# A group-routed residual MLP: dropping reader-less products and laying out every engine's list anew

## The chip, the core and the metric

The kernel runs on one core of a Trainium2 chip. A core has five engines, each with its own queue of instructions, taken in order: TensorE (PE) multiplies matrices, VectorE (DVE) and ScalarE (ACT) work elementwise, GpSimd (POOL) does elementwise work and issues the gathers, and SyncE (SP) issues plain copies (DMA). Engines wait for one another by semaphores. PE writes its products into PSUM, eight banks of 128 x 512 float32 here, which the other engines read. The metric is the device time of one execution, in microseconds (us). Three runs of the kernel before gave 941.57, 938.49 and 941.36 us, median 941.36.

## The reference

There are 16 x 512 = 8192 tokens of width 512. Every token is normalised in several ways, the results are joined and go through a two-layer MLP with a norm behind it, and the input is added:

```python
h = _ln(x, pw_g[pathway_ids], pw_b[pathway_ids])        # gain and bias from one of 500 rows
h = _ln(h, cp_g[compartment_ids], cp_b[compartment_ids])  # of 5 rows
t = _ln(x, tm_g[time_steps], tm_b[time_steps])            # of 5 rows, same ids
m = x + _mlp_ln(memory_state, ...)[:, None, :]            # one row per batch entry
n = x + _mlp_ln(noise_state, ...)[:, None, :]
r = x + _mlp_ln(resource_state, ...)[:, None, :]
s = _ln(x, ms_g[scale_type], ms_b[scale_type])            # scale_type is a 0/1 mask
w = jax.nn.softmax(aw)
cat = jnp.concatenate([w[0]*h, w[1]*t, w[2]*m, w[3]*n, w[4]*r, w[5]*s], axis=-1)
return x + _mlp_ln(cat, int_W1, int_b1, int_W2, int_b2, int_g, int_be)
```

All products are float32, and PE takes a float32 product in two records.

## The kernel before

The tokens are sorted by their group (the pair of time and scale ids) and worked through in 16 tiles of 512 tokens, each four row tiles of 128. The 3072-wide first layer is folded: the parts that are x itself times some weight are summed into one weight (the X block, `wx_`), the two table norms t and s into one weight for each group (the V block, `vs`, rebuilt by ACT and DVE where a row tile's group differs from the one before), and h has its own weight (the H block, `wh_`). The bias rows come from a gather.

For one tile the steps are these. Names such as `q7.p.0.5` are pieces: a kind, the tile, and numbers of a row tile, a pair of row tiles or a product.

- x, h's gain and bias, a compartment row and the bias rows are gathered by POOL (`gx`, `gh`, `gc`, `ga`). ACT and DVE normalise (`xs`, `nv`, `f1`, `fs`, `f2`, `fn`).
- DVE transposes x, v and h in 32 x 32 squares (`tx`, `tv`, `th`, into rX, rV, rH), and SP spreads these to full 128 x 128 transposes by plain copies (`sX`, `sV`, `sH`, four copies for each of four rows, L198) into the turned columns cX, cV, cH.
- PE multiplies: `lV` is the V block of one row tile (8 records of 128 x 512, L392). X and H together are seven half products for each pair of row tiles (`m7.c.pair.1` to `7`, 8 records of 128 x 256 each, L440), after the scheme that saves one product in eight. It needs sums of columns by DVE (`u1` to `u4`, L421 to L427) and sums of products by DVE (`r1`, `r2`, `r3`, `r5`, L451 to L457), which add PSUM banks to the gathered bias rows.
- `ha` (DVE, L460) and `hs` (ACT, silu) make the hidden row tiles; `tz` and `sZ` turn them into cZ.
- The second layer is seven products for each pair of row tiles too (`q7`, L543), with column sums by POOL (`zs`) and sums of products by ACT and DVE (`kf`, `ku`, `sf`, `sl`). Then follow the squares (`lq`), a power by POOL (`lp`), scale and residual (`lb`, two DVE passes, L629 and L630) and the indirect write (`po`, POOL, L634). The last tile takes a plain second layer (`l2`, L475) and a square root on ACT (`sd`, `rv`, `ft`).

The order on every engine is written out by hand in three strings of pieces: ORDER (the head: load, the three conditioning MLPs, tile 0, whose columns PE itself flips, pairs of rows called extras, and the first steps of tile 1), WINDOW (run for tile 0 to 14; p, c, n, m are the tile before, this one, the next and the one after it) and LAST (tile 15). A piece's instructions go to their engines in the order of the strings, nothing is reordered later.

`awake` (L395 to L401) emits a product of 128 x 512 of a weight with itself into a bank that a later product of the list clears. Nothing reads its result. ORDER calls it twelve times, as `wu.lX.0.1.n` into the bank of tile 0's row tile 1 (nine times) and as `wu.ex.n.m` into an extra's bank (three times).

The turned columns live in a pool with one buffer for each of the four blocks. A tile takes the buffer anew at its first copy (`spread_row`, `flipped`, `flipped_extra`), and the head uses parts of it as scratch (`flat_cat`).

## Time and profile before

| | |
|---|---|
| median of three runs | 941.36 us |
| span of the profiled execution | 935.9 us |
| PE busy | 909.9 us, 97% |
| DVE, ACT, POOL busy | 745.0, 502.1, 655.0 us |
| dense products of tile 0 begin | 80.07 us |
| first window's first product | 146.11 us |
| second window | 198.5 to 249.1 us |
| last window's first product | 861.63 us |
| last product ends | 928.1 us |

The time of a run is the span and what lies around it; the profiled execution is shown with its span only, which is 5.5 us under the median. Times inside it count from its start. In the profile a line such as L392 is the line of the kernel, `p<-vs,cV` says what is written and read, and "idle before <-" names what ended an engine's wait. Several parts of one instruction's operands can share a line, since a piece of all tiles has one line. PEclk is the granted clock of PE, as a share of full speed.

### The profile page before, as it was taken

How to read it: one execution, taken by the hardware profiler on the slowest of the kernel's cores; microseconds unless marked ns; L12 is line 12 of the kernel's file. 1: busy time of each engine (PE TensorE's matmuls, PEld its weight loads, DVE VectorE, ACT ScalarE, POOL GpSimd, SP SyncE). 2: the span in 40 equal slices, each digit the busy share in tenths (PEclk: the TensorE clock that was granted, in tenths of full speed). 3: DMA queues.
4: the chain of work that ended last, by engine and by line, in shares of the span. 5: the costliest groups of instructions: out<-in, count | busy, mean ns of one | idle time of the engine just before them, and what ended most of it. 6: DMA issues, size and time to landing. Idle time of an engine off the chain costs nothing. (4 is left out here: it accounts for less than half of the span.)

```text
span 935.9 us, 13631 instructions
## 1 busy us (share of the span) xinstructions
PE 909.9 (97%) x3711; PEld 649.5 (69%) x3711; DVE 745.0 (80%) x1359; ACT 502.1 (54%) x1211; POOL 655.0 (70%) x705
## 2 busy tenths in 40 slices
PE   7999999999999999999999999999999999999996
PEld 6734444877768786868687786878686777767673
DVE  8756776887879697979788786979798987889575
ACT  5557855446372737564654628274656466473322
POOL 9566577667777777677687777776777777775533
PEclk9799999999999999999999999999999999999999
DMA  8856677686867777676868686777777786866613
GB/s 277 256 183 192 181 226 196 185 238 167 247 170 237 189 209 208 194 207 201 237 181 250 165 240 176 219 208 209 204 195 214 201 234 164 247 166 180 185 46 99
DMA packets 88861, 186.68 MB, mean 199 GB/s; under 512 B 24372, under 2 KB 24372, under 8 KB 88780
## 3 DMA queue, kind: packets, MB, share of 16 engines
q0 software_dynamic: 31376, 106.19, 39.9%
q1 hardware_dynamic: 56700, 79.50, 29.2%
q8 instruction: 31, 0.51, 0.3%
q14 instruction: 50, 0.41, 0.1%
q10 hardware_dynamic: 704, 0.08, 0.1%
HBM read 101.78 MB, written 19.94 MB: 130 GB/s over the span
## 5 line engine op out<-in xcount | busy, mean ns | idle before, releaser
L392 PE MATMUL p<-vs,cV 128*128 128x512 f32 x504 | 226.3, 596 | 4.0 <-ACTq L237 2.3
L392 PEld LDWEIGHTS p<-vs,cV 128*128 128x128 f32 x504 | 95.9, 191 | 108.5 <-issue 89.5
L339 ACT ACTIVATE junk<-pw 128x512 bf16<-128x512 f32 x60 | 37.7, 629 | 175.2 <-DVE pw L336 84.9
L440 PE MATMUL p<-wh__80,cH 128*128 128x256 f32 x480 | 111.1, 379 | 0.0
L164 POOL DMA_INDIRECT xbs<-in_x,tok x64 | 69.2, 1081 | 44.4 <-DVE yb L630 24.7
L440 PEld LDWEIGHTS p<-wh__80,cH 128*128 128x128 f32 x480 | 91.2, 190 | 12.4
L634 POOL DMA_INDIRECT out<-yb,tok x64 | 65.4, 1023 | 41.8 <-issue 29.2
L164 POOL DMA_INDIRECT pw<-in_pw,i_pw x64 | 64.7, 1010 | 39.0 <-DVE rH L190 19.9
L164 POOL DMA_INDIRECT cp<-cp_rows,i_cp x64 | 78.8, 1231 | 17.5 <-issue 12.2
L380 POOL TENSOR_TENSOR xbs<-xbs,rows 128x512 f32<-128x512 f32 x64 | 82.2, 1286 | 1.2
L164 POOL DMA_INDIRECT add<-rows,i_add x64 | 67.0, 1048 | 14.7 <-issue 12.5
L361 POOL TENSOR_TENSOR rsh<-veh,mhalf 128x1 f32<-128x1 f32 x64 | 49.2, 768 | 37.2 <-DVE veh L357 32.4
L365 ACT ACTIVATE pw<-pw,rsh 128x512 f32<-128x512 f32 x64 | 44.8, 717 | 53.8 <-issue 23.7
L463 ACT ACTIVATE add<-add 128x512 f32<-128x512 f32 x64 | 38.5, 626 | 63.8 <-DVE add L460 45.4
L335 DVE SCALAR_TENSOR_TENSOR pw<-xbs,sums,pw 128x512 f32<-128x512 f32 x60 | 53.6, 893 | 18.5 <-DMA pw<-in_pw,i_pw 16.2
L372 DVE SCALAR_TENSOR_TENSOR pw<-pw,sumsh,cp 128x512 f32<-128x512 f32 x60 | 44.5, 748 | 18.7 <-DMA cp<-cp_rows,i_cp 7.8
L190 DVE STREAM_TRANSPOSE rH<-pw 128x512 f32<-128x512 f32 x60 | 41.3, 703 | 20.5 <-ACT pw L365 19.8
L440 PE MATMUL p<-wt,cH 128*128 128x256 f32 x240 | 56.7, 379 | 0.0
L440 PE MATMUL u<-wt,ss 128*128 128x256 f32 x240 | 54.5, 380 | 0.4 <-DVE add L454 0.4
L440 PE MATMUL u<-wt,cX 128*128 128x256 f32 x240 | 54.4, 380 | 0.0
L440 PEld LDWEIGHTS u<-wx__79,cX 128*128 128x128 f32 x240 | 45.6, 190 | 12.6 <-issue 5.0
L440 PE MATMUL u<-wx__79,cX 128*128 128x256 f32 x240 | 54.2, 379 | 0.0
(428 smaller groups left out, 2124.2 us busy)
## 6 DMA issues: line engine op xcount, KB each, us to landing
cZ<-rZ SPq DMA_DIRECT2D x256, 64.0 KB
cX<-rX SPq DMA_DIRECT2D x240, 64.0 KB
cV<-rV SPq DMA_DIRECT2D x240, 64.0 KB
cH<-rH SPq DMA_DIRECT2D x240, 64.0 KB
w1x<-in_int_W SPq DMA_DIRECT2D x2, 1024.0 KB
rows<-adde SPq DMA_DIRECT2D x14, 128.0 KB
yb<-in_int_W SPq DMA_DIRECT2D x1, 1024.0 KB
ws<-in_int_W SPq DMA_DIRECT2D x1, 1024.0 KB
```

What stands on the lines that cost most here:

```text
L164: nc.gpsimd.indirect_dma_start(dst, None, table, bass.IndirectOffsetOnAxis(ap=idx, axis=0), **kw)
L190: nc.vector.transpose(rot[:, :, :, j, :].rearrange("p q c t -> p c q t"), src.rearrange("p (c q t) -> p c q t", c=NC, q=Q))
L335: nc.vector.scalar_tensor_tensor(h, st["xb"][:, j, :], st["sums"][:, 1, j : j + 1], h, ALU.add, ALU.mult)
L339: nc.scalar.activation(junk, x, AF.Identity, accum_out=sums[:, 0, k : k + 1])
L361: nc.gpsimd.tensor_tensor(rs, st.pop(("ve", j)), mhalf[:, :1], ALU.pow)
L365: nc.scalar.mul(pw[:, :D], pw[:, :D], st.pop(("rs", j)))
L372: nc.vector.scalar_tensor_tensor(pw[:, :D], pw[:, :D], st["sh", j][:, 1], cp, ALU.add, ALU.mult)
L380: nc.gpsimd.tensor_add(st["xb"][:, j, :], st["xb"][:, j, :], rows[:, 2, :])
L392: nc.tensor.matmul(st["p1", g], st["c" + blk][:, g, c, :], m[:, c, :], start=(blk == first and c == 0), stop=(blk == last and c == NC - 1) ...
L440: nc.tensor.matmul(dst, m[:, c], at_["half1"][k][:, c], start=(k == 1 and c == 0), stop=(c == NC - 1), skip_group_check=True)
L463: nc.scalar.activation(st["add", g], st["add", g], AF.Silu)
L634: nc.gpsimd.indirect_dma_start(out_rows[j], bass.IndirectOffsetOnAxis(ap=tok[:, j, w : w + 1], axis=0), yb[:, j, :], None)
```

## The change

Three things are changed.

1. The twelve `wu` pieces leave ORDER. `awake` stays in the file and is not called.
2. The turned columns are four fixed buffers `cats[blk]` instead of tiles of the pool. A first copy of a tile into the buffer had to wait for all readers of the old tile; a copy into a fixed buffer waits for those of the part it overwrites.
3. ORDER, WINDOW and LAST hold the same pieces as before (but for the twelve) in another order.

```diff
 ORDER = """
-    wk.1.2 h2.1 fx dk lt pk bx sz wk.1.1 by kd wu.lX.0.1.0 xs.0.0 xt.0.0 tk tt wk.1.3 wk.2.1 gx.e0.0 xv.0.0
-    wu.lX.0.1.8 lw fg lo xs.0.1 fl.2 wm.4 h2.2 gx.e0.1 wu.lX.0.1.1 fl.1 scl he.1 xt.0.1 ax he.2 gx.e0.3 gx.e0.2 ac
...
+    wk.1.3 cv wk.1.1 bx fx lt pk h2.1 h2.2 lo by kd tk fg dk wk.1.0 se fl.1 wk.1.2 ax h2.0 dp xt.0.1 tt he.1 fl.2
+    ac he.2 he.0 wm.4 dc xv.0.1 gx.e0.0 xs.0.0 pwi eh.2 gx.e0.1 eh.0 gx.e0.2 sz eh.1 wk.2.3 xs.e0.0 xs.0.1 xs.0.2
...
@@ -145,6 +145,7 @@
     yb = const.tile([P, NJ, D], F32, name="yb")
+    cats = {blk: const.tile([P, Q, NC, P], F32, name="cat" + blk) for blk in "XHVZ"}
     rows = const.tile([P, 3, D], F32, name="rows")
@@ -193,7 +194,7 @@
         if cat not in st:
-            st[cat] = catp.tile([P, Q, NC, P], F32, tag=f"cat{blk}", name=f"{cat}{st['w']}")
+            st[cat] = cats[blk]
@@ -646,7 +647,7 @@
     def flat_cat(blk, name):
-        return catp.tile([P, Q, NC, P], F32, tag=f"cat{blk}", name=name).rearrange("p g c t -> p g (c t)")
+        return cats[blk].rearrange("p g c t -> p g (c t)")
@@ -1118,7 +1119,7 @@
         if "c" + blk not in st:
-            st["c" + blk] = catp.tile([P, Q, NC, P], F32, tag="cat" + blk, name=f"c{blk}{st['w']}")
+            st["c" + blk] = cats[blk]
@@ -1281,7 +1282,7 @@
         if "cE" not in st:
-            st["cE"] = catp.tile([P, Q, NC, P], F32, tag="cat" + "ZX"[k // Q], name="cE" + st["w"])
+            st["cE"] = cats["ZX"[k // Q]]
```

The first place is PE's list in the head, around the turn of the conditioning rows (`pt`), the flips of tile 0 (ptX, ptV) and the conditioning product (`pb`). Before, with the products without a reader (awake):

```order
L401 MATMUL awake_lX_1_563<-wt 128x512
L1211 MATMUL pt<-ident,room_114 128x96 x4
L1117 MATMUL ptX_784<-ident,xbs_90 128x128 x4
L1117 MATMUL ptV_795<-ident,xm_1_765 128x128 x4
L401 MATMUL awake_lX_1_563<-wt 128x512
L1222 MATMUL pb<-yb,room_115 32x512 x4
L1222 MATMUL pb<-w1x_136,room_115 32x512 x4
L1222 MATMUL pb<-w1x_137,room_115 32x512 x4
L1117 MATMUL ptV_821<-ident,xm_2_772 128x128 x4
L401 MATMUL awake_ex_834<-wt 128x512
L1117 MATMUL ptV_845<-ident,xm_0_803 128x128 x4
L1254 MATMUL pr_864<-br,pick 120x512
```

and after the change (lines are one higher there, and the scratch that was `room` is now a part of a fixed buffer, catZ or catH):

```order
L1183 MATMUL pb<-ident,room_118 32x128 x4
L276 UNCONDITIONAL_BRANCH x2
L1212 MATMUL pt<-ident,room_118 128x96 x4
L1118 MATMUL ptX_757<-ident,xbs_90 128x128 x4
L1118 MATMUL ptV_771<-ident,xm_1_745 128x128 x4
L1118 MATMUL ptV_776<-ident,xm_2_739 128x128 x4
L1061 TENSOR_LOAD some
L1223 MATMUL pb<-yb,catZ 32x512 x4
L1223 MATMUL pb<-catH,catZ 32x512 x4
L1223 MATMUL pb<-w1x_139,catZ 32x512 x4
L1118 MATMUL ptV_838<-ident,xm_3_812 128x128 x4
L1118 MATMUL ptV_843<-ident,xm_0_819 128x128
```

The three products without a reader are gone, and three flips of tile 0 stand in one row ahead of the conditioning product.

The second place is SP's list where the head ends and the first window begins: cX and cV are tile 1's turned columns, `rows_78<-adde` are the extras' row copies, and the branches belong to parts that run only for a changed group. Before:

```order
L1311 DMA rows_78<-adde_1290 64x512 x2
L1311 DMA rows_78<-adde_1161 64x512 x2
L198 DMA cX_1389<-rX_1138 32x512
L237 UNCONDITIONAL_BRANCH
L198 DMA cX_1389<-rX_1138 32x512 x4
L237 UNCONDITIONAL_BRANCH
L198 DMA cX_1389<-rX_1138 32x512 x7
L198 DMA cV_1474<-rV_1298 32x512 x7
L237 UNCONDITIONAL_BRANCH x2
L198 DMA cV_1474<-rV_1298 32x512
L237 UNCONDITIONAL_BRANCH
L198 DMA cV_1474<-rV_1298 32x512 x3
```

and after:

```order
L1312 DMA rows_78<-adde_1366 64x512
L238 UNCONDITIONAL_BRANCH x2
L1312 DMA rows_78<-adde_1366 64x512
L238 UNCONDITIONAL_BRANCH
L199 DMA catV<-rV_1327 32x512 x9
L238 UNCONDITIONAL_BRANCH
L199 DMA catV<-rV_1327 32x512 x6
L238 UNCONDITIONAL_BRANCH
L199 DMA catV<-rV_1327 32x512
L199 DMA catX<-rX_1084 32x512
L238 UNCONDITIONAL_BRANCH
L199 DMA catX<-rX_1084 32x512 x7
```

Twelve copies of cX stood ahead of the first copy of cV; now all sixteen copies of cV stand ahead of the last eight of cX.

The third place is DVE's list in the window of tile 2, from the last of the output pairs (yb, lines 629 and 630, in the new file 630 and 631) to the sum r2 into add_0 (line 451, new 452). u_0 is the bank that the first pair's products 1, 6 and 7 share; catX and catH are written by the token sums u3 and u4, pw is the next tile's h. Before:

```order
L453 TENSOR_TENSOR add_0_2032<-add_0_2032,u_0_1994 128x256
L454 TENSOR_TENSOR add_1_2126<-add_1_2126,u_0_1994 128x256
L427 TENSOR_TENSOR cH_2092<-cH_2092,ss_2208 128x512
L425 TENSOR_TENSOR cX_1866<-cX_1866 128x512
L453 TENSOR_TENSOR add_2_2150<-add_2_2150,u_1_1989 128x256
L454 TENSOR_TENSOR add_3_2171<-add_3_2171,u_1_1989 128x256
L629 SCALAR_TENSOR_TENSOR yb<-yb,rsy,rows 128x512
L630 TENSOR_TENSOR yb<-yb,xbs_88 128x512
L451 TENSOR_TENSOR add_0_2032<-add_0_2032,u_0_1994 128x256
```

and after:

```order
L373 SCALAR_TENSOR_TENSOR pw_0_2080<-pw_0_2080,sumsh,cp_0_2144 128x512
L630 SCALAR_TENSOR_TENSOR yb<-yb,rsy,rows 128x512
L631 TENSOR_TENSOR yb<-yb,xbs_88 128x512
L336 SCALAR_TENSOR_TENSOR pw_1_2148<-xbs_90,sums,pw_1_2148 128x512
L337 SCALAR_TENSOR_TENSOR pw_1_2148<-pw_1_2148,rsx 128x512
L426 TENSOR_TENSOR catX<-catX 128x512
L428 TENSOR_TENSOR catH<-catH,ss_2204 128x512
L454 TENSOR_TENSOR add_0_1991<-add_0_1991,u_0_1953 128x256
L455 TENSOR_TENSOR add_1_2146<-add_1_2146,u_0_1953 128x256
L238 UNCONDITIONAL_BRANCH
L452 TENSOR_TENSOR add_0_1991<-add_0_1991,u_0_1953 128x256
```

Before, the sums r5 (two rows that begin L453 and L454) and the token sums of both pairs stand ahead of the last output pair; now the output pair, an h pass (L373) and front_1 (L336, L337) stand ahead of them. WINDOW's PE list has the seven half products in another order too: before, 0.2, 0.4, 0.5, 1.5, 0.6, 1.6, 0.7, 1.7, 1.2, 0.3, 1.4, 1.3 after the first two (pair and product), now 1.2, 0.5, 1.3, 0.2, 1.6, 0.6, 1.5, 0.4, 0.7, 0.3, 1.7, 1.4.

In LAST the plain second layer of the last tile takes its row tiles in the order 0, 3, 1, 2 instead of 0, 2, 1, 3, and its end stands so: before `la.c.3 ft.c.2 lq.c.3 sd.c.3 yg.c.3 po.c.1 rv.c.3 ft.c.3 po.c.2 po.c.3`, now `la.c.2 lq.c.2 lq.c.3 sd.c.2 sd.c.3 po.c.1 sh.c.2 yg.c.3 rv.c.2 yg.c.2 rv.c.3 ft.c.2 ft.c.3 po.c.2 po.c.3`.

90 lines of the change are left out of this document (45 added, 45 removed).

## The prediction

> **What bounds the kernel now.** I read the page first, then PE's waits, then the busy time by stage, and last the two ends of the program instruction by instruction.
>
> ```profile
> span 935.9 us, 13631 instructions
> PE 909.9 (97%) x3711; PEld 649.5 (69%) x3711; DVE 745.0 (80%) x1359; ACT 502.1 (54%) x1211; POOL 655.0 (70%) x705
> PEclk9799999999999999999999999999999999999999
> ```
>
> PE (TensorE) is busy for 97% of the span and runs at full clock in nearly all slices, so whatever changes the time must either take products away, close a gap of PE, or open one. The median of the runs shown is 941.4 us: 5.5 more than this execution's span, and I take those 5.5 as unchanged.
>
> ```profile
> PE p L392 <- ACTq L237: 2.3, 1, 2.3
> PE pq_0a L543 <- DVE yb L559: 1.0, 1, 1.0
> PE pq_1b L543 <- DVE yb L561: 0.7, 1, 0.7
> PE pq_0b L543 <- POOL cZ L522: 0.4, 1, 0.4
> ```
>
> These are PE's waits in the tiles' products (us in total, times, longest): one of 2.3 us, and a handful of about 1 us, each met once. They are too few to be of the repeated window. The stages:
>
> ```profile
> core 0: us, PE busy (x) PEld busy (x) DVE busy (x) ACT busy (x) POOL busy (x), PEclk, DMA share, GB/s
> 38.00:47.50 9.50, 9.50 (x53) 5.45 (x51) 7.25 (x26) 1.88 (x6) 3.80 (x5) 0.50 0.65 218
> 47.50:80.00 32.50, 29.66 (x186) 12.39 (x186) 17.93 (x57) 20.75 (x48) 19.14 (x19) 1.00 0.56 186
> 80.00:143.80 63.80, 62.22 (x161) 27.95 (x159) 48.87 (x89) 44.76 (x94) 43.94 (x44) 1.00 0.69 202
> ...
> 146.10:150.00 3.90, 3.89 (x5) 1.63 (x6) 1.41 (x3) 0.00 (x0) 3.13 (x4) 0.56 0.92 259
> ...
> 198.50:249.10 50.60, 50.60 (x205) 38.07 (x204) 42.12 (x75) 27.33 (x68) 37.74 (x39) 1.00 0.74 207
> 249.10:861.60 612.50, 609.61 (x2449) 455.13 (x2448) 509.39 (x906) 338.06 (x820) 450.59 (x452) 1.00 0.73 205
> ...
> 906.00:928.20 22.20, 21.05 (x64) 11.21 (x62) 14.00 (x25) 8.73 (x22) 10.82 (x11) 1.00 0.36 106
> ```
>
> The second window (198.5 to 249.1) is PE without a gap: 50.60 us is the floor of a window. The next twelve take 612.5, 51.04 each, so only 12 x 0.44 = 5.3 us are above the floor. The loop has nothing much to win and a factor of 14 to lose. What can be won lies ahead of 146.1 (the first window's start) and behind 906.
>
> **Part 1: the twelve products without a reader.** Their groups, and the second of the twelve in time:
>
> ```profile
> L401 PE MATMUL awake_lX<-wt 128*128 128x512 f32 x18 | 11.1, 711 | 0.0
> L401 PE MATMUL awake_ex<-wt 128*128 128x512 f32 x6 | 3.2, 610 | 0.0
> ```
>
> ```profile
> 46.33 1.59 PE L401 MATMUL awake_lX<-wt 128*128 128x512 f32 x2
> ```
>
> 24 records (two to a product) are 14.3 us of PE, all but the first two products in the stretch from 47.5 to 80. Without those 10/12 x 14.3 = 11.9 us PE has 29.7 - 11.9 = 17.8 us of work in that stretch of 32.5, so PE no longer sets its length, and the products are not worth 14 us either: the others still have ACT 20.75, POOL 19.14 and DVE 17.93 us to do. The end of the stretch, where the dense products of tile 0 start, reads:
>
> ```profile
> 73.89 1.00 POOL L164 DMA_INDIRECT pre<-diff_rows,tok_x  x1 [0.18 <-PE pr L1254]
> 78.07 0.60 ACT L1123 COPY cV<-ptV 128x512 f32<-128x512 f32 x1
> 78.55 0.61 ACT L1123 COPY cX<-ptX 128x512 f32<-128x512 f32 x1
> 79.21 1.02 PE L401 MATMUL awake_ex<-wt 128*128 128x512 f32 x2
> 80.07 1.88 PE L392 MATMUL awake_lX<-wx__79,cX 128*128 128x512 f32 x4
> ```
>
> The dense start at 80.07 waits for the last flipped column of x, copied by ACT until 79.2. In the new list that flip stands behind fewer products and its copy behind fewer pieces. How much earlier? No row shows it, so by bounds. Earliest: ACT never idle from 47.5 on, 47.5 + 20.75 = 68.3, and 2.4 more for a weight build of ACT that the new list has moved ahead of the start: 70.7. (2.4 is an estimate: four ACT passes over a 128x512 tile at 0.60, the copy above.) Latest: no earlier than 80.07. Following the new lists through with the old durations I get the last pair row landing at about 70 and its flip, the last h flip and the first dense product at 73.5. That is nearer to the early end, and I take it: **-6.6** (ends -9.4 and 0).
>
> The dense phase itself has the same products, 62.2 us busy in 63.8. Of the 1.6 idle I let half remain (-0.8, ends -1.6 and +3, should a gather come late for an earlier start). Its clock is the other risk: the row from 146.1 shows what a clock of half costs, 0.56 in the mean over 3.9 us, that is 1.7 us of lost progress. With PE two thirds busy ahead of it, the dense phase may begin so: +0.8, half of that (ends 0 and +1.7).
>
> **Part 2: the copies into the turned columns (SP), and the first window.**
>
> ```profile
> 129.07 8.35 SPq L198 DMA_DIRECT2D cX<-rX  x12
> 137.54 8.00 SPq L198 DMA_DIRECT2D cV<-rV  x12
> 145.58 2.49 SPq L198 DMA_DIRECT2D cX<-rX  x4
> ```
>
> SP issues 12 copies in 8.35 us, 0.7 each (0.67 and 0.62 in the other rows), without a pause from 129.07 to 148. The first window's first product needs row 1 of V, the second of the three V rows that begin at 137.54, and so PE stands for the 2.3 us. The profile's name for the releaser, ACT's sequencer, is the branch around a weight build that was not taken; the copy is the later of the two. In the new list the four V rows stand right behind the extras' last row copies, two X rows are issued between those copies, and the other two X rows, first read two products into the window, come last; with fixed buffers a row waits for the readers of its own row alone. By the walk V row 1 is issued 10 us or more before the window. The stall goes: **-2.3** (ends -2.3 and 0). With it goes the half clock behind it, 3.9 x (1 - 0.56) = **-1.7** (ends -1.7 and 0). What is late next there is V row 0: SP issues it last of the four, 12 x 0.67 = 8 us behind row 1, and PE reads it one product later, which is 3.6 us (the product of 924.54, below). That takes 4.4 us of the lead of 10.
>
> [...]
>
> **Part 3: the repeated window.** All lists are rewritten; the same instructions run. For each wait of PE I walked the new order with the old durations. Most keep over 1.5 us. The thinnest is the seventh half product of the first pair, which overwrites a bank that DVE must have read (the row sums r5 and r2). The rates:
>
> ```profile
> 542.04 0.74 DVE L629 SCALAR_TENSOR_TENSOR yb<-yb,rsy,rows 128x512 f32<-128x512 f32 x1
> 542.82 0.69 DVE L630 TENSOR_TENSOR yb<-yb,xbs 128x512 f32<-128x512 f32 x1
> 543.42 0.41 DVE L451 TENSOR_TENSOR add<-add,u 128x256 f32<-128x256 f32 x1
> 543.75 0.76 DVE L335 SCALAR_TENSOR_TENSOR pw<-xbs,sums,pw 128x512 f32<-128x512 f32 x1
> 544.55 0.75 DVE L336 SCALAR_TENSOR_TENSOR pw<-pw,rsx 128x512 f32<-128x512 f32 x1
> 545.22 0.41 DVE L451 TENSOR_TENSOR add<-add,u 128x256 f32<-128x256 f32 x1
> 545.69 2.11 PE L440 MATMUL u<-wt,cX 128*128 128x256 f32 x9
> 547.63 3.62 PE L440 MATMUL p<-wh__80,cH 128*128 128x256 f32 x16
> ```
>
> From start to start an output pair (L629, L630) is 1.38 us, a 256-wide add 0.33, front_1 (L335, L336) 1.47, another full pass about 0.65; a half product is 8 records in 8 x (547.63 - 545.69) / 9 = 1.72 us. Before, three output pairs stood ahead of r2, and front_1 and the h pass behind it. Now four pairs, the h pass, front_1, two token sums and r5 (two adds) stand between the sum u4 of the other pair and r2: 4 x 1.38 + 0.65 + 1.47 + 1.3 + 0.66 + 0.33 = 9.9 us behind u4, which itself takes 0.65. PE has seven half products in that time, 7 x 1.72 = 12.0 us, counted from the end of m7.1.2, which frees what u4 writes; by the walk u4 begins about 1 us after that. So 12.0 - 1.0 - 0.65 - 9.9 = 0.45 us are left. That is positive, but one late start of an output pair, which waits for a power of POOL, would use it. The fixed buffers cost nothing here: SP is idle between the h rows and the V rows already, and starts the z rows at the old time. The weight builds of changed groups now have more room (lV.3 stands two products later), the only gain left. I take **+1.0** for 14 windows (ends -5.3, where the excess above the floor goes, and +13, where one more output pair in the way, 1.38 - 0.45 = 0.93, is lost in each).
>
> **Part 4: the last window's end.**
>
> ```profile
> 924.54 3.60 PE L475 MATMUL p<-w,cZ 128*128 128x512 f32 x8
> 928.18 0.69 DVE L603 TENSOR_TENSOR yb<-p,rows 128x512 f32<-128x512 f32 x1
> 928.90 0.63 ACT L608 ACTIVATE junk<-yb 128x512 bf16<-128x512 f32 x1 [1.06 <-DVE yb L603]
> 929.66 0.29 ACT L584 ACTIVATE sd<-ssy,eps 128x1 f32<-128x1 f32 x1
> 930.24 0.75 DVE L599 SCALAR_TENSOR_TENSOR yb<-yg,sd,xbs 128x512 f32<-128x512 f32 x1
> 931.27 0.96 POOL L634 DMA_INDIRECT out<-yb,tok  x1 [0.31 <-DVE yb L599]
> ```
>
> After the last product (928.15) one row tile is added, squared, rooted, scaled and written: the write starts 3.1 us on. In the new list two row tiles share that chain: ACT squares both before either root, DVE scales both before either sum, and the last write stands behind another write of POOL. Added (0.7), square of 2 (0.8), of 3 (0.8), two roots (0.5), the rest of DVE to the first sum (0.8 + 0.75), first write 1.2 from start to start: the last write starts at 5.6 to 5.8. **+2.6** (ends 0 and +3). Against it the second half's products of layer 2 are in an order that meets DVE's and POOL's sums later, the 0.7 and part of the 1.0 and 0.4 in the waits above: **-1.3** (ends -2.1 and 0).
>
> Sum: -6.6 - 0.8 + 0.8 - 2.3 - 1.7 + 1.0 + 2.6 - 1.3 = **-8.3**, against 935.9 + 5.5 = 941.4: 933 us.
>
> **Rivals.**
> 1. *The start hardly moves.* The dense start hangs on the pair rows, gathered by POOL (73.89 above) and turned, and not on PE's queue; POOL, at 19.1 of 32.5 us, has order left to lose. Then only the stall and its clock are won: 941.4 - 4.0 + 1.3 = 938.7, and with +1 of the loop 939.7. For it: POOL's gathers wait for indices that PE's, ACT's and DVE's chain makes. Against it: that chain runs through PE behind five of the dropped products.
> 2. *The clock.* Without the dropped products PE is 17.8 / 32.5 = 55% busy at full clock; if it stays at half from 38 on (0.50 in the first row of the stages), the 17.8 us are 35.6, and the dense start is at 47.5 + 35.6 = 83.1, 3 us later than now, with 1.7 more until the clock is back: 941.4 + 3.0 + 1.7 - 4.0 + 2.3 = 944.4. Against it: at half clock PE would be busy without a gap, and after 9.5 us of that the clock came back at 47.5 in this trace. [...]
> 3. *Slower: DVE late in each window.* POOL's power for the output pairs stands behind gathers in POOL's queue, 1.0 us each (73.89). Two of them in the way make r2 late by 2.0 - 0.45 = 1.55 us, and PE stands so long at the seventh half product of 14 windows: 941.4 - 9.3 + 14 x 1.55 = 954. It decides from 9.3 / 14 = 0.66 us per window: from there the whole gain is gone. For it: DVE has 42.1 of 50.6 us of work and five more full passes ahead of that read. Against it: POOL is less loaded than DVE (37.7 of 50.6), and the same work was in the window before.
> 4. *More than I take.* The loop's excess goes and the start lies at 71: 933 - 6.3 - 2.5 = 924.
>
> **How the numbers follow.** My forecast (929 to 937) gets 0.48, rival 4 0.08, rival 1 0.13, rival 2 0.07, rival 3 0.24. A measurement of this kernel cannot tell less than about 0.3% (2.8 us) from no change: faster is under 938.5, slower over 944.2. Of rival 1 I count 0.08 as faster and 0.05 as same, of rival 2 0.03 as same and 0.04 as slower, of rival 3 0.02 as faster (a loss under 0.45 us a window), 0.02 as same and 0.20 as slower. Faster: 0.48 + 0.08 + 0.08 + 0.02 = 0.66; same: 0.05 + 0.03 + 0.02 = 0.10; slower: 0.04 + 0.20 = 0.24. The range leaves about 1 in 10 on either side: 923 below (rival 4), 949 above (rival 3 with 1.2 us a window). My forecast's own range is 929 to 937.
>
> **What would show it.** Right: the dense products of tile 0 start at 71 to 76; no wait of PE over 1 us at the first window, which starts at 134 to 139; granted clock 1.0 from there on; window starts 50.6 to 51.2 apart; 5 to 6 us from the last layer-2 product to the last write. Wrong: windows of 51.8 and more, with PE waiting for DVE's adds of L451 (L452 in the new file) or token sums; a granted clock of 0.5 between 50 and 90; a dense start near 80 behind pair rows. The first of these alone would turn the sign.

## The result, and the profile after

The changed kernel takes 948.5 us (median of 6 runs, 943.4 to 954.9) beside 937.9 us for the kernel before (6 runs, 933.9 to 941.6): a ratio of 1.011, 95% interval 1.007 to 1.015. It is slower by about 1%; faster, 933 us, was forecast. Lines of the new file are one higher than before (L441 for the half products, L458 for the sum r3, L461 for the hidden sums, L199 for SP's copies, L544 for the second layer).

From the page of the changed kernel, its totals, PE's clock and the chain that ended last:

```profile
span 947.6 us, 13773 instructions
PE 899.1 (95%) x3687; PEld 643.8 (68%) x3687; DVE 748.7 (79%) x1359; ACT 498.0 (53%) x1211; POOL 657.2 (69%) x705
PEclk9989999999999999999999999999999999999998
...
PE 16%; SPq 4%; POOL 2%; DMA 2%; DVE 2%; issue 2%; ACT 0%; POOLq 0%; DVEq 0%; ACTq 0%
```

PE's busy time fell by 10.8 us (the dropped products had been 14.3), but the span grew by 11.7. The chain, which can be followed back to 668 us here, has 4% of the span, 38 us, in SP's queue. (The chain of the kernel before can be followed back to 870 us only, the last window, so the two shares cannot be set side by side.) PE's waits in the tiles' products (us in total, times, longest):

```profile
PE pq_0a L544 <- POOL catZ L523: 7.3, 5, 1.6
...
PE pq_0a L544 <- DMA catZ<-rZ: 6.7, 11, 1.4
...
PE pq_0a L544 <- DVE yb L560: 2.8, 3, 1.0
PE pq_0a L544 <- POOL zs L521: 1.6, 1, 1.6
```

Before, these were single waits of about 1 us. Now two places recur: the first z product (`q7.p.0.1`) waits for the copies into catZ, and the sixth (`q7.p.0.6`) for what is summed from catZ (three of the four rows; which engine is late last varies). By stages (us, PE's busy time, the other engines', granted clock, DMA share, GB/s):

```profile
47.50:73.00 25.50, 17.87 (x120) 10.15 (x120) 20.57 (x59) 21.01 (x46) 17.62 (x19) 0.87 0.61 204
73.00:135.00 62.00, 59.56 (x153) 26.47 (x152) 46.48 (x86) 41.09 (x90) 45.67 (x44) 1.00 0.75 230
135.00:187.70 52.70, 52.70 (x211) 39.03 (x210) 43.32 (x74) 25.18 (x62) 39.42 (x40) 1.00 0.69 196
187.70:872.70 685.00, 664.95 (x2654) 492.99 (x2652) 556.52 (x980) 362.24 (x887) 488.68 (x489) 1.00 0.70 199
```

The fourth row is the thirteen windows from the second one's start to the last one's: 685.0 us, 52.69 each. Before, the same thirteen took from 198.50 to 861.63, 51.01 each. So the account of the profiled executions is: second window's start 187.68 for 198.50, -10.8; thirteen windows +21.9; from the last window's start to the end 74.86 for 74.26, +0.6. Together +11.7, the difference of the spans. The head won what was forecast, and the loop lost it twice over.

The head in rows of the timeline (start us, us). PE at the dense start:

```profile
72.50 0.63 PE L1118 MATMUL ptH<-ident,pw 128*128 128x128 f32 x4 [0.48 <-ACT rows L1259]
72.97 2.31 PE L393 MATMUL p<-wx__79,catX 128*128 128x512 f32 x5
```

SP at the end of the head:

```profile
121.43 2.64 SPq L1312 DMA_DIRECT2D rows<-adde  x4
124.17 10.44 SPq L199 DMA_DIRECT2D catV<-rV  x16
134.66 5.05 SPq L199 DMA_DIRECT2D catX<-rX  x8
```

PE where the first window begins (137.23):

```profile
131.65 5.74 PE L393 MATMUL p<-wh__80,catH 128*128 128x512 f32 x13
137.23 7.03 PE L393 MATMUL p<-vs,catV 128*128 128x512 f32 x16
```

The dense products begin at 72.97 behind the last h flip, and the first window at 137.23 without a wait and at full clock: the V copies are issued from 124.17 on.

Now the loop. This is the chain of the changed kernel from the end of one window (start us, us, what) through the next, which starts at 714.69, into the one after, which starts at 765.98:

```profile
704.67 0.61 DVE catX L426
705.30 0.51 SPq L199
...
713.56 5.33 DMA catX<-rX
718.91 0.68 SPq L199
...
721.44 4.16 DMA catZ<-rZ
725.59 0.14 issue
725.73 1.97 PE pq_0a L544 x8
...
764.41 1.73 PE p L441 x8
766.14 1.73 PE p L393 x4
767.87 0.30 SPq L199
...
771.52 1.26 SPq L199
...
782.24 1.97 DMA catZ<-rZ
```

DVE's last writing into the old x columns (the token sum u3) releases SP's copies of the next x columns; SP issues them, the four copies of V row 0 that now stand between them, and behind them the z copies, on which PE stands at 725.73. One x copy is 5.33 us under way here, and SP stands for its landing (in the built program each of SP's copies waits until the copy eight before it has landed; such waits for x copies are 6.4 us in 8 in this trace, 1.9 at the most). In the next window the chain passes from PE to SP: the last four x copies wait for the last half product that reads x (`m7.c.1.7`). Its records end 1.56 us ahead of the window's start, at 764.42, and SP goes on at 767.87, 3.4 us later.

DVE sees the same. Its third difference (`r3`, L458) waits for the same product. In the timeline around the window that starts at 558.29 the product, on PE, is

```profile
554.84 1.89 PE L441 MATMUL u<-wt,catX 128*128 128x256 f32 x8
```

the sum on DVE, with its idle time and what ended it,

```profile
559.08 0.69 DVE L458 TENSOR_TENSOR add<-add,u 128x512 f32<-128x512 f32 x1 [2.78 <-PE p L441]
```

and SP's copies

```profile
548.91 2.41 SPq L199 DMA_DIRECT2D catX<-rX  x4
551.37 2.51 SPq L199 DMA_DIRECT2D catV<-rV  x4
553.97 8.27 SPq L199 DMA_DIRECT2D catX<-rX  x12
564.23 10.00 SPq L199 DMA_DIRECT2D catZ<-rZ  x16
```

The product's records end at 554.84 + 1.89 = 556.73; DVE, idle for 2.78 us, starts at 559.08, 2.35 us later. Behind r3 in DVE's queue stand the four hidden sums and four turns of the z rows, the last two of which read

```profile
562.68 1.49 DVE L191 STREAM_TRANSPOSE rZ<-add 128x512 f32<-128x512 f32 x2
```

They are done at 564.17, 5.9 us into the window; SP's x copies had ended at 562.24, and its z copies start at 564.23, right behind the last turn, as in 11 of the 14 windows. The first z product is due 10.3 us in.

### The profile page after: what moved, and what is told of

Read it like the earlier page. It is cut to its first block, busy times and chain, and to the rows that moved or that the text cites. A ratio compares the mean times of both kernels' runs of the same rounds, so it can differ in the third digit from the quotient of the medians.

```text
span 947.6 us, 13773 instructions
## 1 busy us (share of the span) xinstructions
PE 899.1 (95%) x3687; PEld 643.8 (68%) x3687; DVE 748.7 (79%) x1359; ACT 498.0 (53%) x1211; POOL 657.2 (69%) x705
## 5 line engine op out<-in xcount | busy, mean ns | idle before, releaser
L393 PE MATMUL p<-vs,catV 128*128 128x512 f32 x512 | 227.6, 592 | 0.1
L393 PEld LDWEIGHTS p<-vs,catV 128*128 128x128 f32 x512 | 97.1, 190 | 104.1 <-issue 93.0
L441 PE MATMUL p<-wh__80,catH 128*128 128x256 f32 x480 | 110.9, 379 | 0.0
L441 PEld LDWEIGHTS p<-wh__80,catH 128*128 128x128 f32 x480 | 91.2, 190 | 18.4 <-issue 6.7
L165 POOL DMA_INDIRECT pw<-in_pw,i_pw x64 | 64.4, 1006 | 28.6 <-issue 13.7
L381 POOL TENSOR_TENSOR xbs<-xbs,rows 128x512 f32<-128x512 f32 x64 | 81.7, 1279 | 1.0
L165 POOL DMA_INDIRECT cp<-cp_rows,i_cp x64 | 69.0, 1078 | 17.3 <-issue 14.7
L165 POOL DMA_INDIRECT add<-rows,i_add x64 | 64.8, 1013 | 16.4 <-issue 14.1
L307 ACT ACTIVATE xm<-xbs,nmx,rsx 128x512 f32<-128x512 f32 x64 | 49.0, 808 | 24.1 <-DVE nmx L301 13.4
L441 PE MATMUL u<-wt,catX 128*128 128x256 f32 x240 | 56.6, 379 | 0.1
L441 PE MATMUL p<-wt,catH 128*128 128x256 f32 x240 | 56.7, 379 | 0.0
L441 PE MATMUL u<-wx__79,ss 128*128 128x256 f32 x240 | 56.5, 379 | 0.0
L336 DVE SCALAR_TENSOR_TENSOR pw<-xbs,sums,pw 128x512 f32<-128x512 f32 x60 | 53.8, 897 | 2.6 <-DMA pw<-in_pw,i_pw 1.3
L441 PE MATMUL u<-wt,ss 128*128 128x256 f32 x240 | 54.4, 379 | 0.0
L441 PE MATMUL u<-wx__79,catX 128*128 128x256 f32 x240 | 54.4, 379 | 0.0
```

What stands on the lines that cost most here:

```text
L165: nc.gpsimd.indirect_dma_start(dst, None, table, bass.IndirectOffsetOnAxis(ap=idx, axis=0), **kw)
L307: nc.scalar.activation(t, st["xb"][:, j, :], AF.Identity, bias=st["nm"][:, j : j + 1], scale=st["rs"][:, j : j + 1])
L336: nc.vector.scalar_tensor_tensor(h, st["xb"][:, j, :], st["sums"][:, 1, j : j + 1], h, ALU.add, ALU.mult)
L381: nc.gpsimd.tensor_add(st["xb"][:, j, :], st["xb"][:, j, :], rows[:, 2, :])
L393: nc.tensor.matmul(st["p1", g], st["c" + blk][:, g, c, :], m[:, c, :], start=(blk == first and c == 0), stop=(blk == last and c == NC - 1) ...
L441: nc.tensor.matmul(dst, m[:, c], at_["half1"][k][:, c], start=(k == 1 and c == 0), stop=(c == NC - 1), skip_group_check=True)
```

## The experiments

The mean is over the thirteen windows from the second's start to the last's; ratios are to runs of the kernel before on the same chip. "start" is the dense start. The record puts e1 to e8 on chip 13, e9 to e11 on chip 3, e12 to e15 on chip 4 and e16 to e18 on chip 0, and names no chip for the changed kernel. The kernel before, timed along with them, took 938.9 (e1 to e4), 938.4 (e5 to e8), 937.3, 934.4 and 932.7 us, so runs of different chips are compared by their ratios.

| run | edit | us | ratio, 95% interval | start | mean window |
|---|---|---|---|---|---|
| before | | 937.9 | | 80.07 | 51.01 |
| after | | 948.5 | 1.011 [1.007, 1.015] | 72.97 | 52.69 |
| e1 | after, WINDOW of before | 1058.9 | 1.127 [1.125, 1.130] | 73.13 | 60.33 |
| e2 | before, WINDOW of after | 1040.6 | 1.108 [1.105, 1.110] | 79.98 | 58.83 |
| e3 | before without the products | 933.6 | 0.994 [0.992, 0.996] | 78.17 | 50.90 |
| e4 | after, r3 later | 947.5 | 1.009 [1.006, 1.012] | 74.47 | 52.32 |
| e5 | after, lV.3 ahead of z | 949.8 | 1.011 [1.004, 1.018] | 73.55 | 52.62 |
| e6 | after, sums fed earlier | 952.4 | 1.011 [1.003, 1.020] | 73.98 | 52.92 |
| e7 | e5 and e6 | 975.7 | 1.039 [1.034, 1.044] | 73.68 | 54.55 |
| e8 | e7 and r3 later | 976.3 | 1.039 [1.035, 1.044] | 73.62 | 54.60 |
| e9 | after, POOL's shift later | 942.4 | 1.008 [1.005, 1.011] | 73.25 | 51.98 |
| e10 | after, turn not behind r3 | 945.6 | 1.012 [1.006, 1.019] | 74.37 | 52.20 |
| e11 | e9 and e10 | 951.7 | 1.016 [1.011, 1.020] | 73.43 | 52.66 |
| e12 | after, four copies earlier | 925.5 | 0.990 [0.987, 0.993] | 72.30 | 50.90 |
| e13 | e10 and e12 | 927.0 | 0.991 [0.987, 0.995] | 72.02 | 51.18 |
| e14 | e9, e10 and e12 | 924.0 | 0.991 [0.988, 0.994] | 70.96 | 50.82 |
| e15 | before, ORDER of after | 943.2 | 1.010 [1.006, 1.014] | 72.46 | 51.01 |
| e16 | e12 and lV.3 ahead of z | 924.0 | 0.990 [0.986, 0.993] | 72.52 | 50.66 |
| e17 | e14 and lV.3 ahead of z | 926.9 | 0.993 [0.991, 0.995] | 72.66 | 51.02 |
| e18 | as e12 | 924.8 | 0.991 [0.989, 0.993] | 72.49 | 50.84 |

### Whole parts of the change apart: e1, e2, e3, e15

e1 puts the old WINDOW into the changed kernel.

> The changed kernel (no reader-less products, fixed buffers, new head and new end) with the repeated window's list of the kernel before. If the whole loss is in the new order of the window: windows go back from 52.7 to about 51.0 us, and the start keeps its gain (dense products of tile 0 at 73 instead of 80), so 7 to 11 us under the kernel before, about 928. If the loss comes from the fixed buffers or from how the head leaves the queues, the windows stay at 52 to 53 and the time stays near 947.

It took 1058.9 us, with PE in 14 waits of 7 us each (98.0 us) for the copies into catX. With fixed buffers the list's order decides what a reader reads: the old list names the x copies of the next tile ahead of the last readers of the old columns, and those then read the next tile's, so the x part of some half products is not the one of the reference here (PE's waits for these copies fit this; which products read wrong columns is not shown). The old list cannot stand on the new buffers.

e2 puts the new WINDOW into the kernel before.

> The kernel before with only the window's list exchanged for the new one; head, end, the twelve products and the pool buffers stay. If the window's order alone makes the loss: 14 windows at 52.7 to 53.3 us, 20 to 25 us over the kernel before, about 960. If the new window is only bad behind the new head, it is near the kernel before.

1040.6 us: PE waits 22.8 us for copies into cV and 15.7 and 9.1 us around cZ. With tiles of the pool the first copy of a block waits for all readers of an old tile, and the new list has copies of several blocks interleaved. Neither list can be judged without its buffers.

e3 drops the twelve products alone.

```diff
-    wu.lX.0.1.8 lw fg lo ...
+    lw fg lo ...
```

> The kernel before without the twelve reader-less products, all else as it was. If they stood in the way of the flips of tile 0 (the prediction's part 1): dense products begin 3 to 7 us earlier, and the time falls by 3 to 7 us. If other engines bound the stretch: under 1 us. If the clock needs them: PE at half clock somewhere between 50 and 90 us and the time 0 to 4 us longer.

The dense start moves by only 1.9 us (to 78.17), and the products are worth 0.6% of the time: 934.3 us is the profiled span, 1.6 less than before, and the median is 5.3 less. The rest between these two is not traced. What brought the dense start to 73 is the new order of the head, and e15 takes that alone: the kernel before with ORDER of the changed one, and WINDOW, LAST and buffers of before.

> The kernel before, with its own columns from the pool, its own list for the windows and for the end, and the changed kernel's list for the head (which leaves the twelve products out). If the loss lies in the windows' list alone and the gain in the head's, the dense phase starts near 73 us and the windows keep 50.5 us: 80.1 - 73.0 = 7 us less and the first window's wait and half clock gone, 926 to 932 us. If the new head only pays with the new windows' list (its first window being handed over in another state), the dense start moves but the time stays at 933 to 938 us.

The dense start is at 72.46, and the time is 943.2: slower than before. The longest of PE's waits in e15, and SP's rows at the end of its head:

```profile
PE p L391 <- DVEq L236: 14.1, 3, 13.7
```

```profile
136.16 2.52 SPq L1310 DMA_DIRECT2D rows<-adde  x4
138.78 11.08 SPq L197 DMA_DIRECT2D cV<-rV  x16
```

The first window waits 13.7 us; SP, whose first x copy into a tile of the pool must wait for the readers of the old tile (19.4 us in one wait, which the profile puts to the extras' products on PE), issues the V rows 14.6 us later than the changed kernel (138.78 for 124.17). So the head's gain needs the fixed buffers: new order and buffers belong together.

### PE's two waits, taken away one by one: e4 to e8

First theory: the two waits of each window are the whole loss, and giving each more slack removes it. e4 moves r3 behind the work that follows it on DVE, e5 puts 3.4 us of V products ahead of the first z product, e6 lets the sums that the sixth waits for start earlier, e7 does the last two, e8 all three.

```diff
 e4
-    ... ha.c.1 r3.c.1 ha.c.0 ... sX.n.1 ha.c.3
+    ... ha.c.1 ha.c.0 ... sX.n.1 r3.c.1 ha.c.3
 e5
-    ... sp.c.2 q7.p.0.1 q7.p.0.2 lV.c.3
+    ... sp.c.2 lV.c.3 q7.p.0.1 q7.p.0.2
 e6
-    ... fn.c.2 fn.c.3 xs.n.1 xs.n.2 kf.p.0 ... xe.n gh.n.0 zs.p.2
+    ... kf.p.0 fn.c.2 fn.c.3 xs.n.1 xs.n.2 ... xe.n zs.p.2 gh.n.0
```

> The changed kernel with one piece of the window moved: DVE's sum r3 of the second pair, which waits for the last-but-one half product, goes behind the hidden row tiles 1 and 0 and the first turn, where only row tile 3 needs it. Theory: this wait holds up all of DVE at the window's end, the z columns are turned 1.5 us late, and PE's stalls at the first second-layer products follow from that. Then the z copies start 1 to 1.5 us earlier, windows are 51.5 to 52.3 instead of 52.7 and the time falls by 6 to 16 us. Rival: the stall of the sixth product comes from its own place in PE's list (it is asked for before its sums are there); then windows stay within 0.3 us of 52.7.

> The changed kernel with one product moved in the window's PE list: the V block of row tile 3 (3.4 us) goes back ahead of the first two second-layer products, where the list before had it. Theory: PE asks for the first z row 3.4 us too early, and the wait for the z copies (6.7 us in all in the profile, up to 1.4 a window) goes away. Then 5 to 8 us under the changed kernel, about 941 to 943. Rival: the second wait of the window (the sixth product, 1.6 us) has the same cause, the late turn of z, and takes over what the first gives back; then the time falls by less than 3 us and the sixth product's wait grows.

> The changed kernel with two pieces of the window moved: ACT copies the first second-layer product out ahead of the h norms and two x sums instead of behind them, and POOL forms the third z sum ahead of a gather. These two feed the sixth second-layer product. Theory: that product's wait (11.7 us in all in the profile, 1.6 us in most windows) comes from these queues; it goes away: 8 to 13 us under the changed kernel, about 936 to 940. Rival: the sums wait for the z copies themselves; then the wait stays within 0.3 us a window.

> Both moves together (V block of row tile 3 back ahead of the first z product; the sixth product's sums fed earlier). If the two waits are the whole loss of the window: windows at 50.7 to 51.2 us, 18 to 22 us under the changed kernel, so about 927 to 930 and 9 to 12 us under the kernel before. If a ring of waits through DVE, SP and PE sets the window's length: other waits appear and windows stay above 52 us.

> Both moves and the sum r3 of the second pair later on DVE (as in the run with that move alone). If the late turn of z still costs something with both waits fed: 1 to 4 us under the run with both moves. If the slack is enough without it: the same within 0.3%.

The theory fell. e4 takes 0.4 us off the mean window and 1.0 us off the time, where 6 to 16 us were expected. In e5 the first wait is gone and the sixth product's stays, in e6 it is the other way round, and the mean window is 52.6 and 52.9 as before the edit. In e7 both old waits are gone and new ones stand in each window, for ACT's and DVE's writing of yb (21.0 us in 14 and 13.6 us in 12): 975.7 us. e8, with r3 later too, gains nothing on that (976.3). A wait removed at PE came back at another product, which pointed to a ring of engines that sets the period and that PE's wait only closes.

### The ring: e9, e10, e11

Second theory: the ring runs from the late r3 through the turn of the z rows (DVE), the z copies and z sums, and POOL's shift (`sh.c.0`, L381), beside which a pass of DVE over h lasts up to 2.2 us instead of 0.74. e9 moves the shift away from that pass, e10 puts three of the four turns ahead of r3, e11 does both.

```diff
 e9
-    ... gc.c.3 ga.c.0 sh.c.0 bd.c.3 ... zs.p.7 sh.c.3
+    ... gc.c.3 ga.c.0 bd.c.3 ... zs.p.7 sh.c.3 sh.c.0
 e10 (pair 1 of tile c; the fourth turn opens the next window as tz.p.3)
-    ... ha.c.1 r3.c.1 ha.c.0 ... hs.c.1 hs.c.0 tz.c.1 sV.n.1 ... sX.n.1 ha.c.3 hs.c.3 tz.c.0
+    ... ha.c.1 ha.c.0 ha.c.2 ... hs.c.1 hs.c.0 hs.c.2 tz.c.1 tz.c.0 tz.c.2 sV.n.1 ... sX.n.1 r3.c.1 ha.c.3 hs.c.3
```

> The changed kernel with one piece moved on POOL: the addition to x of row tile 0 (1.28 us) goes behind that of row tile 3, out of the window's first 8 us, where it ran beside DVE's first pass over h and that pass took 2.2 us instead of 0.72. Theory of the ring (row sums r3, turn of z, h passes, x sums, sums of the second layer, sixth product, all in one circle round the window): every microsecond taken out of the ring shortens the window by as much, here 1.46 us in the 6 of 13 windows that showed it: 6 to 9 us under the changed kernel, about 940 to 942. Rival (waits that are not one ring, each with its own cause): under 3 us.

> The changed kernel with DVE's list at the window's end in another order: hidden row tiles 1, 0 and 2 and their turns first, then the sum r3 of the second pair, and behind it only row tile 3 (the silu of row tile 2 goes ahead likewise). In the profile DVE stood 2.6 to 4.4 us before that sum and eight of its passes (5 us) stood behind it. Ring theory: the chain behind the sum falls from 5.1 to about 2.7 us, more than the 2.1 us that the window is over the floor of 50.6: windows at 50.7 to 51.3, 19 to 27 us under the changed kernel, about 922 to 929, and faster than the kernel before. Rival: the copies of x by SP, which end 4 us into the window, or ACT's queue hold the rest; then 5 to 10 us.

> Both of these moves. Ring theory: the ring has slack by then, the windows are at the floor but for the weight builds: within 3 us of the run with the turn alone, about 922 to 927. Rival: if the turn alone leaves a stall, this takes up to 8 us more off.

e9 is 6 us under the changed kernel in the medians, as expected, but by the ratios (1.008 for 1.011, with intervals that overlap) the gain is not clear of noise. e10 took away the sixth product's wait and no time that the ratio shows (922 to 929 was expected); both together gave nothing. So the ring theory's sums did not come. In the window of e10 that starts at 554.35, DVE's last turn ends at 557.68, 3.3 us in, but SP's rows there read:

```profile
550.40 8.94 SPq L199 DMA_DIRECT2D catX<-rX  x12
559.98 10.02 SPq L199 DMA_DIRECT2D catZ<-rZ  x16
```

SP's x copies end at 559.34, 5.0 us into the window, and the z copies start at 5.6. In this window SP, not DVE, kept the z copies. That pointed at SP, which the chain of the changed kernel had named too.

### SP's copies: e12, e13, e14, e18

In the changed kernel SP stands for u3 of DVE (72.7 us in 14 waits, 5.2 a window) ahead of the x copies, with V row 0's four copies behind that wait though their source is ready. Third theory, with two branches: the z copies are held by two chains, DVE's turn and SP's x copies, so that both must go (A), or SP alone sets them (B). e12 is one piece of 189, moved by one place; e13 is e10 with the same edit, e14 adds e9.

```diff
-    ... sV.n.1 sV.n.3 sV.n.2 sX.n.0 sV.n.0 sX.n.2 sX.n.1
+    ... sV.n.1 sV.n.3 sV.n.2 sV.n.0 sX.n.0 sX.n.2 sX.n.1
```

> The changed kernel with one edit on the DMA queue that SyncE issues: the four copies sV.n.0 stand ahead of the x copies instead of between the first four and the other twelve. In the changed kernel SyncE waits 5.2 us a window for VectorE's last writing into the x columns (72.7 us in 14 waits) with these four copies (2.5 us) behind that wait, and its x copies end 4.0 us into the next window; the z copies begin at 5.9 us, because VectorE's turn of the z rows ends there. Theory A (two chains meet at the z copies: VectorE's turn at 5.9 us and SyncE's x copies at 4.0 us; the turn is the later one in this kernel): the x copies end about 2.5 us earlier, nothing else moves, mean window 52.3 to 52.7 us, time within 3 us of the changed kernel (945 to 951). Theory B (SyncE's x copies alone set the z copies): mean window 50.9 us, about 925 us.

> The turn ahead of VectorE's third difference (as in e10) and the four copies sV.n.0 ahead of the x copies, together. In e10 VectorE's turn ended at 3.3 us, but SyncE's x copies ended at 5.0 us of the window and the z copies began at 5.6 us. Theory A (two chains meet there, either one alone keeps the z copies late): with both removed the z copies begin at about 3.5 us and PE's wait for them goes; mean window 50.8 to 51.2 us and a time of 924 to 931 us, below the kernel before. Theory B (the ring is closed by something else, such as the landing of the copies or PE's late completions): mean window stays at 52 us or more, 943 us or more.

> The same as e13 and in addition GpSimd's shift behind the half product's later work (as in e9), so that VectorE's first pass over the h rows does not run beside it. Theory A: no more than 1 us better than e13, since the sixth product's wait was gone in e10 already; 923 to 931 us. Theory B: as e11, 951 us.

e12 alone gives 925.5 us, the number of branch B: 1% under the kernel before on the same chip. Under the changed kernel it is 23.0 us in the medians and, by the ratios (0.990 for 1.011), about 19 us; but those two did not run on the same chip, and what that leaves open is said below. Its span, from the page, and its stage from the second window's start to the last's, the counterpart of the 685.0 above:

```profile
span 923.8 us, 13775 instructions
```

```profile
187.28:848.96 661.68, 658.01 (x2653) 494.38 (x2652) 555.78 (x978) 363.56 (x887) 489.05 (x490) 1.00 0.73 206
```

That is 23.3 us less than in the changed kernel: 16.4 of PE's idle time (20.05 to 3.67) and 6.9 of its busy time for the same work (in the changed kernel the 208 records of `u<-wt,catX` have a mean of 380 ns and keep PE busy for 49.2 us together, 237 ns each, so neighbouring records overlap; the sixth product's 52 records, with 11.7 us of waits, are busy for 14.0 us, and for 13.4 in e12, with 0.3 us of waits; whether the like is all of the 6.9 is not shown). Nearly the whole difference of the spans (23.8) lies in these windows. The rows of e12 that answer to those of the window at 558.29, here at 494.51, again of PE, DVE and SP:

```profile
491.06 1.89 PE L440 MATMUL u<-wt,catX 128*128 128x256 f32 x8
```

```profile
492.98 0.69 DVE L457 TENSOR_TENSOR add<-add,u 128x512 f32<-128x512 f32 x1 [1.07 <-PE u L440]
```

```profile
485.06 11.11 SPq L198 DMA_DIRECT2D catX<-rX  x16
498.13 10.07 SPq L198 DMA_DIRECT2D catZ<-rZ  x16
```

```profile
496.58 1.49 DVE L190 STREAM_TRANSPOSE rZ<-add 128x512 f32<-128x512 f32 x2
```

The x copies end at 496.17, 1.7 us into the window instead of 3.95, as the edit was to bring about. The z copies start 3.6 us in instead of 5.9. But they start right behind DVE's last turn (498.07), here and in every window of e12, 0.9 us or more after the x copies ended: so SP's x copies do not set them, as branch B had it, although its number came. DVE's turn sets them, as in A, and the turn is early because r3 starts at 492.98, 0.03 us behind the product's end of 492.95, instead of 2.35; from r3's start to the end of the last turn it is 5.09 us in both kernels. r3 is so prompt in 11 of the 14 windows of e12 (in the other three DVE itself is busy until later), where in the changed kernel it came 1.7 to 3.4 us late in ten windows, was kept by DVE's own work in three, and was prompt in the last alone. A was wrong in that nothing else would move. e13 and e14, with the turn and the shift moved as well, are no better than e12 within their intervals.

That the moved piece made PE's signal prompt is not shown, and the record speaks against it. The traces hold the moment at which each signal of PE (the update of a semaphore that other engines wait for) arrives. Call one late when it comes more than 0.06 us behind the last record end that could have sent it. Between 185 and 870 us the changed kernel's trace has 41 late ones, that of the kernel before 19, that of e3 11, and those of e4 to e11 have 22 to 61 each (e1 and e2, with windows of 59 to 60 us, have none). None of e12 to e18 has any. Among these is e15, which has the windows and the buffers of the kernel before and not the moved piece. What e12 to e18 have in common, and no other traced run has, is the chips, 4 and 0. (Of the first group's traces 18 to 26% of the records of PE's signals are missing, of the second's about 1% at most; so the first counts can be too low.) No run has the window of the changed kernel without the moved piece on chip 4 or 0. How much of the 23 us is the piece and how much the chip is therefore open.

An estimate from e12's own rows makes the piece the smaller part. With the V copies back in between, its x copies would end 2.5 us later, 3.8 us into most windows, 0.2 us behind the turn's end at 3.6; and in the window of e12 at 645.85, where the z copies start 1.5 us later than in most, PE waits 0.3 us for them. The late r3 moved the turn by 2.3 us.

Why PE's signal comes late in some traces is not settled. These rows have the load on the DMA engines in the 4 us ahead of a window's start (the last three columns are the clock, the DMA share and GB/s), in the changed kernel (window at 558.29), in e12 (494.51) and in the kernel before (554.54):

```profile
554.29:558.29 4.00, 4.00 (x21) 3.51 (x19) 1.89 (x3) 0.78 (x2) 3.38 (x4) 1.00 0.89 257
```

```profile
490.51:494.51 4.00, 4.00 (x21) 3.51 (x19) 2.91 (x6) 0.91 (x3) 3.30 (x4) 1.00 0.79 237
```

```profile
550.54:554.54 4.00, 4.00 (x20) 3.51 (x19) 2.83 (x6) 1.29 (x3) 2.71 (x3) 1.00 0.79 229
```

The share is 0.89 in the changed kernel and 0.79 in e12, but 0.79 also in the kernel before, whose trace has late signals; in the next 4 us it is 1.01, 0.99 and 0.90. So the load alone does not tell the traces with late signals from those without. e18 was to separate how long SP is at its copies from where V's copies stand, by issuing the first four x copies twice:

> e12 with the first four x copies of a window issued a second time, behind the second four: SyncE has as many copies ahead of the last eight x copies as in the changed kernel (2.5 us more), but the V copies stand ahead of all x copies as in e12. The copies repeat the same rows, so nothing computed changes. Theory A (how long SyncE is at its x copies, and what its copies load on the DMA engines at the window's end, sets the late releases and the z copies): the x copies end about 4 us into the window again, VectorE's third difference starts up to 3 us behind the product again, mean window 52 us or more, 943 us or more. Theory B (it is the place of the V copies as such, their landing late or their wait): as e12, 924 to 930 us.

It separates nothing. A second mention of a piece in the list issued nothing, the trace has 16 x copies a window as in e12, and the run is a repetition of e12: 924.8 for 925.5.

### What is left: e16, e17

```diff
-    ... sp.c.2 q7.p.0.1 q7.p.0.2 lV.c.3
+    ... sp.c.2 lV.c.3 q7.p.0.1 q7.p.0.2
```

> e12 (the copies sV.n.0 ahead of the x copies) and, on PE, the 16 matmuls lV.c.3 ahead of the first z product (as in e5), which gives the z copies 3.4 us more. In e12 PE waits 0.3 to 1.3 us for the z copies in three of 14 windows and loses 2.9 and 0.5 to 0.7 us in others; the floor is 50.45 us. Theory A (the z copies are the only thing left to wait for): windows of 50.45 us throughout but for one or two, 918 to 923 us. Theory B (the sixth z product's sums come next, as in e5, where this move brought nothing): 925 us or more.

> e14 (copies, turn and shift) and lV.c.3 ahead of the first z product. Theory A: 917 to 922 us, all windows near 50.45 us, since both the z copies and the sums have slack. Theory B: 924 us or more, something else takes the place.

On e12 the move of e5 removes the wait for the z copies for good, and nine of the thirteen windows of e16 take 50.45 us; with 924.0 for 925.5 the two cannot be told apart. On e14 it gives 926.9, and waits of DVE and POOL are back. A floor of 13 x 50.45 = 655.9 us stands against 658.6 in e16: the loop has no more to give to a move of this kind. e12, e14 and e16 beat the kernel before on their own chips by about 1%; beside the changed kernel on one chip none of them was run.

## Why the prediction was right and wrong

- *Part 1, the dense start* (-6.6): 72.97, that is -7.1; right, and inside 71 to 76. It is mostly not the work of the dropped products (e3: -1.9) but of the new order. The dense phase's share, -0.8 + 0.8, came out so too: from the dense start to the second window's start it is 114.7 us for 118.4, 3.7 less, beside the 4.0 of part 2.
- *Part 2, the first window* (-2.3 and -1.7): right. No wait there, no half clock. With part 1 the start was to win 10.6; it won 10.8. Rivals 1 and 2 did not come. The granted clock of 0.5 between 50 and 90, listed as a sign of being wrong, did: 0.50 from 57.2 to 63.9, which makes 0.87 in the mean from 47.5 to 73. The dense start was not late for it.
- *Part 4, the end* (+2.6 - 1.3 = +1.3): +0.6 measured. From the last product's end (937.15) to the last write's start (943.04) are 5.9 us, 5.6 to 5.8 were forecast.
- *Part 3, the repeated window* (+1.0, upper end +13): wrong, +21.9 in thirteen windows. The step that failed is the sentence that the fixed buffers cost nothing, since SP "starts the z rows at the old time". SP started the z rows 5.9 us into the window; in the kernel before, 4.4 us (558.98, with the window at 554.54). SP's own list is not what made them late: its x copies end 3.95 us into the window, with the copies of V row 0 now among them, and 3.86 us into it before (558.40). Late was DVE's turn of the z rows behind r3. In the kernel before, the half product that r3 waits for (the last in the first of these rows, on PE), r3 itself, the last turns and SP's copies read

```profile
544.83 2.97 PE L440 MATMUL u<-wt,cX 128*128 128x256 f32 x13
```

```profile
553.85 0.68 DVE L457 TENSOR_TENSOR add<-add,u 128x512 f32<-128x512 f32 x1
557.43 1.49 DVE L190 STREAM_TRANSPOSE rZ<-add 128x512 f32<-128x512 f32 x2
```

```profile
547.83 10.57 SPq L198 DMA_DIRECT2D cX<-rX  x16
558.98 10.00 SPq L198 DMA_DIRECT2D cZ<-rZ  x16
```

There the product's records end at 547.80, 6.05 us ahead of r3. In the new list of PE this product (`m7.c.1.7`) stands last but one, DVE stands for it, and r3 got the signal up to 3.4 us behind the product's end. The walk took PE's results as reaching DVE and SP with the end of the product, and put nothing for this; without late signals, and with the copies of V row 0 moved, the same orders of PE and DVE have windows of 50.90 (e12) and 50.84 us (e18). Why the signals were late here stays open.
- *The thinnest place*: the 0.45 us at the seventh half product never turned into a wait of PE in the changed kernel. What stood behind "most keep over 1.5 us" was thinner: the first z product, moved from 13.8 to 10.3 us into the window.
- *Rival 3* had the sign and nearly the size (954), by another mechanism: POOL's power and DVE's r2 were not late. So its 0.24 was not earned by its reasons, and the price list had no row for a sum that gets its product's signal late.
- *The base*: 941.4 was the median of three runs, and the 5.5 us around the span belonged to those runs. Around the span of the changed kernel's profiled run lie 949.5 - 947.6 = 1.9 us, and over six runs the kernel before takes 937.9. That moves a forecast of 933.0 to 929.6 for the same reasons, and the measured size of the change is to be taken to 937.9.

With the one piece moved (e12), the gain over the kernel before is 8.9 us (925.5 beside 934.4 in the same runs); -8.3 was forecast for the change. That the two are so near bears nothing out: e12 ran without late signals, and how the changed kernel does without them was not measured.

## What to carry to other kernels

A sum that follows its product at once in the lists is a thin place even if the product's recorded end is in time: here up to 3.4 us passed between that end and the sum, and what stood behind the sum was late by as much. A queue that only issues copies is an engine of the schedule too: walk its order in the repeated part as one walks DVE's, and look at each window for which of the chains that meet at a copy ends last. Run the control with the experiment: the largest gain here (e12) cannot be put to its edit, because the changed kernel was not run again on that chip. And a fixed buffer and the order written for it are one change: each half alone was slower than nothing (e1, e2, e15).

## What the runs showed of the hardware beside that

- *In these traces a product's records can end long before its readers go on.* In e12 r3 starts 0.03 us behind the product's last record, in ten windows of the changed kernel 1.7 to 3.4 us, and the runs of chips 4 and 0 have no late signal in their windows; SP goes on as late as DVE in the chain shown above (3.4 us). So a matmul's recorded end was not its release here; where the lag comes from is not shown.
- *DVE beside POOL.* A pass of DVE that reads two tensors (L336, 128 x 512) takes 0.73 us in the mean of 51 in the changed kernel, and 1.83 us in the mean of the nine that ran beside POOL's addition of L381, 2.2 us at the most. All nine end 0.56 us behind the end of the addition. In six of the nine DVE's record starts first, by 0.1 to 0.4 us, in the other three 0.4 to 0.7 us behind the addition's start. A pass that begins near the addition's end loses little: in the kernel before, 22 of the 30 that overlap it take 0.70 to 0.86 us. The walk of part 3 took 0.74 for all of them.
- *The clock.* Without the twelve products PE ran at 0.87 of full clock from 47.5 to 73 while only 17.87 of 25.5 us busy, and at 1.00 from 73 to 918; before, the same stretch had 1.00 (from 38 to 47.5 it was the other way round, 0.82 now and 0.50 before). The clock that the products bought was worth less than the products: without them alone (e3) the clock is 0.83 from 47.5 to 78.2, and the time is 0.994 of before.
